# A bidirectional selective scan: one scan instruction for both states of a step, with the seam set up by ScalarE, and GpSimd operands in pairs

## The chip, the cores and the metric

The kernel runs on one core of a Trainium2 chip. A core has five engines with queues of their own: TensorE (PE, matrix products and transposes), VectorE (DVE), ScalarE (ACT), GpSimd (POOL) and SyncE (SP, which here issues DMAs). Each queue is worked off in order; engines wait for each other through semaphores. SBUF is the working memory, 128 partitions wide. PSUM is a smaller one in eight banks of 512 f32 a partition, into which PE writes, and which ACT and DVE read and write too. The metric is the device time of one execution, in microseconds (us).

## The reference, cut to what matters

The input is x of 2 sequences, 2048 tokens, 256 channels, in f32. It passes a layernorm with a modulation, then two Mamba blocks, one forward and one over the reversed sequence, then a mixture of eight experts with a shared one. The change lies in the Mamba blocks alone. Of each, cut:

```
xp, z = split(x @ W_in.T)                    # 512 channels each
xc    = silu(conv(xp) + b_conv)              # 4 taps along the tokens
dt, B, C = split(xc @ W_x.T, [16, 32])       # 16 states: B and C have 16 values a token
dt    = softplus(dt @ W_dt.T + b_dt);  A = -exp(A_log)
step: h = h * exp(dt * A) + (dt * xc) * B    # h: 512 channels x 16 states
      y = sum over the states of h * C
y     = (y + xc * D) * silu(z);  out = y @ W_out.T
```

The recurrence over the tokens is what the kernel's scans compute: for each channel and each state, h[t] = da[t] * h[t-1] + db[t], with da = exp(dt * A) and db = (dt * xc) * B.

## The kernel before, in words

A direction and a sequence are cut in chunks of 512 tokens, which makes 16 chunks (2 directions, 2 sequences, 4 chunks). Channels lie on the partitions in four blocks d of 128; tokens lie along the free axis. The 16 states are taken in eight groups g of two (NG = 2). A *step* is one group of one channel block: two states, 512 tokens each. A chunk has SPC = 32 steps, ordered by pair of blocks p, then g, then block e within the pair; s is the number of a step, over all chunks 0 to 511. Step numbers below are within a chunk.

A step passes these functions:
- `load_b`, `load_c` (SP): rows of B and C of a group, spread over 128 partitions by DMA, once for two steps.
- `inputs` (POOL, L416): db = du * B for both states, 128 x 1024 into a tile of SBUF with ten slots; du is dt * xc (`input_`, L306).
- `decays` (ACT, L435): da = exp(dt * a), one ACTIVATE for each state, 128 x 512 each into a PSUM bank of its own. Even and odd steps have two banks each (`banks`).
- `scans` (DVE, L449): one TENSOR_TENSOR_SCAN for each state, starting from the state `hl` that the chunk before left.
- `weigh_own` (DVE, L455) or `weigh` (POOL, L460): h * C. `on_pool` says which: POOL has the odd blocks but for one group, and steps 4 and 16. For steps on POOL the scan writes h to SBUF; for the others it writes h over the decays in PSUM.
- `carry` (ACT, L470 or L466): the last column of h is copied to hl.
- `sums` (PE, L482): transposes that add up h * C over the states in PSUM; `gate_y` (DVE, L500) multiplies by the gate.

In four *turned* steps of a chunk (6, 7, 18, 19; not in the first chunk) POOL makes no db. PE does it instead, with transposes of scaled du (`scaled`, `operands`, tile op) into the PSUM banks, and the decays go to SBUF.

The order on each engine is written by hand in the loop over s. In one iteration are issued: `load_b`, `weigh(s-2)`, `load_c`, `inputs(s+3)`, `carry(s-1)`, perhaps a softplus, `gate_y(s-5)`, `scans(s)`, `weigh_own(s)`, `decays(s+1)`, `operands(s+1)`, then evacuations of PE's products by ACT (`settle`), `sums(s-4)`, and work for the next chunk that `places` puts at fixed steps (`visit`). Of this, the steps of the prediction touch: the silu of the convolution at step 12 and of the gate at 28 (L242 and L246, each with two table loads on ACT), the product psd at 14 (PE, L253) and its evacuation xd (L258), the four ACTIVATEs ab (L336), the evacuation xT (L209) with the products psx (L219) behind it, and the softplus of the next chunk at steps 20, 22, 24 and 26. A softplus (`softplus_in` on ACT, L292 and L293; `softplus_out` on DVE, L298 to L300) borrows the two PSUM banks of step s+1 before that step's decays are written there.

Of the kernel before, what the change touches and what calls it, by code (L numbers as in the profile page):

```python
# [40 lines left out]
def kernel(  # L41
# [30 lines left out]
    nc.vector.memset(one, 1.0)  # L72

# [4 lines left out]
    def tiled(ap):  # L78

        return ap.rearrange("(j p) c -> p j c", p=P)  # L80

# [16 lines left out]
    with tc.tile_pool(name="mw", bufs=1) as mw, tc.tile_pool(name="mw2", bufs=2) as mw2, \  # L98
# [59 lines left out]
        def on_pool(s):  # L158

            i, _, g, d = steps[s]  # L160
            if i == 0:
                return d % 2 == 1 and g not in (NGR - 4, NGR - 2)
            return s % SPC in (4, 16) or d % 2 == 1 and g != NGR - 2
# [121 lines left out]
        def banks(s, name):  # L285

            return [ps_a.tile([P, TC], F32, tag=f"da{s % 2}_{n}", name=f"{name}_{n}") for n in range(NG)]

        def softplus_in(i, d, s):
            v = ready[i]  # L290
            v["sl"] = banks(s, f"sl{i}_{d}")
            nc.scalar.activation(v["sl"][0], v["e"][:, d, :], AF.Identity, bias=one)  # L292
            nc.scalar.activation(v["sl"][1], v["e"][:, d, :], AF.Ln, bias=one)  # L293

        def softplus_out(i, d):
            v = ready[i]
            (s, ln), e, dt = v["sl"], v["e"][:, d, :], v["dt"][:, d, :]
            nc.vector.scalar_tensor_tensor(e, s, -1.0, e, ALU.add, ALU.subtract)  # L298
            nc.vector.tensor_tensor(ln, ln, e, ALU.subtract)
            nc.vector.scalar_tensor_tensor(dt, dt, 0.0, ln, ALU.max, ALU.add)  # L300
# [111 lines left out]
        def inputs(s):  # L412
            i, _, g, d = steps[s]
            db = m2.tile([P, NG, TC], F32, tag="db", bufs=NDB, name=f"db{s}")
            if not turned_step(s):
                nc.gpsimd.tensor_tensor(db, bc(ready[i]["du"][:, d, :], NG), live["B", s // 2], ALU.mult)  # L416
            live["db", s] = db

        def operands(s):

            if turned_step(s):
                i, _, _, d = steps[s]
                live["op", s] = banks(s, f"op{s}")
                for n, op in enumerate(live["op", s]):
                    for j in range(JC):
                        transpose(op[:, j * P:(j + 1) * P],
                                  ready[i]["ab"][:, n, j, d % 2 * P:(d % 2 + 1) * P], ident)

        def decays(s):
            i, _, g, d = steps[s]  # L430
            w = weights[chunks[i][0]]
            da = [live["db", s][:, n, :] for n in range(NG)] if turned_step(s) else banks(s, f"da{s}")
            for n in range(NG):
                m = g * NG + n
                nc.scalar.activation(da[n], ready[i]["dt"][:, d, :], AF.Exp, scale=w["a"][:, d, m:m + 1])  # L435
            live["da", s] = da

        def scans(s):
            i, _, g, d = steps[s]
            hl, da = state[chunks[i][:2]][0], live.pop(("da", s))  # L440
            x = live.pop(("op", s)) if turned_step(s) else [live["db", s][:, n, :] for n in range(NG)]
            h = x if turned_step(s) else da
            if on_pool(s):
                live["h", s] = m2.tile([P, NG, TC], F32, tag="h", bufs=3, name=f"h{s}")
                h = [live["h", s][:, n, :] for n in range(NG)]
            live["hs", s] = h
            for n in range(NG):
                m = g * NG + n
                nc.vector.tensor_tensor_scan(h[n], da[n], x[n], hl[:, d, m:m + 1], ALU.mult, ALU.add)  # L449

        def weigh_own(s):
            _, _, g, d = steps[s]
            if not on_pool(s):
                for n, h in enumerate(live["hs", s]):
                    nc.vector.tensor_tensor(live["db", s][:, n, :], h, live["C", s // 2][:, n, :], ALU.mult)  # L455

        def weigh(s):
            _, _, g, d = steps[s]
# [3 lines left out]
        def carry(s):  # L462
            i, _, g, d = steps[s]
            hl, hs = state[chunks[i][:2]][0], live.pop(("hs", s))
            if on_pool(s):
                nc.scalar.copy(hl[:, d, g * NG:(g + 1) * NG].unsqueeze(2), live["h", s][:, :, TC - 1:TC])  # L466
            else:
                for n in range(NG):
                    m = g * NG + n
                    nc.scalar.copy(hl[:, d, m:m + 1], hs[n][:, TC - 1:TC])  # L470
# [125 lines left out]
        def load_x(b, q):  # L596
            xt = m2.tile([P, JC, C], F32, tag="db", bufs=NDB, name=f"xt{b}_{q}")
            nc.sync.dma_start(out=xt, in_=tiled(x[b, q * TC:(q + 1) * TC, :]))
            return xt

        def norms(b, q, xt, xn):
# [17 lines left out]
            if xn is None:  # L619
                xn = m2.tile([P, JC, C], F32, tag="db", bufs=NDB, name=f"xo{u}")  # L620
# [20 lines left out]
        front = norms(0, 0, xts[0, 0], xns[0])  # L641
# [39 lines left out]
        def others():  # L681
# [3 lines left out]
            while todo or live:  # L685
                while todo and len(live) < 2:
                    k = todo.pop(0)
                    live.append(norms(*k, xts.pop(k), None))
# [50 lines left out]
        for s in range(3):  # L739
            inputs(s)  # L740
# [28 lines left out]
        for s in range(NST + 4 + SPC):  # L769
# [8 lines left out]
            if s + 3 < NST:  # L778
# [550 lines left out]
```

## Time and profile before

| | us |
|---|---|
| median of 11 runs | 2473.47 (2470.28 to 2479.17) |
| the profiled execution | 2472.45, span 2470.7 |
| first scan starts / last scan ends | 103.3 / 1892.3 |
| a usual chunk, first scan to first scan | 109.2 |
| DVE, POOL, ACT, PE busy in such a chunk | 106.4, 107.3, 85.6, 91.2 |

A group of the profile is a line, an engine, an operation and tiles (out<-in, buffer numbers left out), with the size of one, the count, the busy time in us and the mean duration in ns, then the engine's idle time just before and what ended it. A row of the timeline has start, duration, engine, line, operation and tiles, and in brackets idle time before it and its releaser. The window row has the window, its length, then busy time (and count) of PE, PEld (weight loads), DVE, ACT and POOL, the granted clock of TensorE as a share of full speed, the DMA share and GB/s. Instructions of one engine overlap at their ends, so the sum of durations is above busy time; distances between starts are what an instruction costs in a full queue.

### The profile page before, as it was taken

The page shows a single profiled execution, that of the slowest core. Times are in us where ns is not written, and L with a number is a line of the kernel's source. Part 1 is how long each engine was busy: PE and PEld are TensorE (multiplying, and loading weights), DVE is VectorE, ACT ScalarE, POOL GpSimd, SP SyncE. Part 2 cuts the span into 40 slices and gives each one's busy share as a digit, 9 for nine tenths or more (in the row PEclk, how much of TensorE's full clock was granted, in tenths as well). Part 3 has the DMA queues.
Part 4 walks back from the last instruction along what each step waited for, and adds up shares of the span by engine and source line. Part 5 has one row for each costly group of instructions (what it writes and reads, how often), then busy time and mean ns, then how long its engine had stood idle before and what let it go on. Part 6 is the DMA issues. An engine that isn't in the chain of part 4 may idle for free. (4 is left out here: it accounts for less than half of the span.)

```text
span 2470.7 us, 30346 instructions
## 1 busy us (share of the span) xinstructions
PE 1986.5 (80%) x9512; PEld 1373.3 (56%) x9512; DVE 2031.0 (82%) x2679; ACT 1625.2 (66%) x3377; POOL 1886.0 (76%) x991
## 2 busy tenths in 40 slices
PE   5457879787887879788887978888765487999999
PEld 2134556565555556555555656555555255788885
DVE  5499998999999999999999999999996776322333
ACT  5557787777778787877878777787853235353331
POOL 0367998989999999999999999999996405331304
PEclk9687888898999889899988989899878688999999
DMA  5344448474444454545444544444443501688863
GB/s 165 129 145 146 145 163 252 154 248 166 155 162 164 147 188 165 170 158 167 155 154 163 165 162 152 167 156 148 164 153 99 173 1 63 203 261 239 270 187 102
DMA packets 239974, 403.08 MB, mean 163 GB/s; under 512 B 38818, under 2 KB 171938, under 8 KB 239812
## 3 DMA queue, kind: packets, MB, share of 16 engines
q1 hardware_dynamic: 220724, 370.72, 46.1%
q0 software_dynamic: 6144, 16.79, 2.0%
q10 hardware_dynamic: 12944, 13.64, 1.6%
q8 instruction: 75, 1.23, 0.2%
q14 instruction: 87, 0.71, 0.1%
HBM read 346.54 MB, written 54.53 MB: 162 GB/s over the span
## 5 line engine op out<-in xcount | busy, mean ns | idle before, releaser
L416 POOL TENSOR_TENSOR db<-du,B 128x1024 f32<-128x1024 f32 x452 | 1062.4, 2371 | 13.8 <-DMA B<-bcs 13.8
L460 POOL TENSOR_TENSOR db<-h,C 128x1024 f32<-128x1024 f32 x252 | 597.0, 2370 | 65.8 <-issue 52.6
L435 ACT ACTIVATE da<-dt,w_a 128x512 f32<-128x512 f32 x904 | 594.7, 688 | 76.8 <-DVE dt L300 46.2
L482 PE MATMUL y<-ident,db 128*128 128x128 f32 x4096 | 569.3, 287 | 39.2 <-POOL db L460 36.6
L482 PEld LDWEIGHTS y<-ident,db 128*128 128x128 f32 x4096 | 506.1, 150 | 160.6 <-issue 101.1
L449 DVE TENSOR_TENSOR_SCAN da<-da,hl,db 128x512 f32<-128x512 f32 x460 | 562.8, 1268 | 4.9 <-POOL db L416 3.7
L449 DVE TENSOR_TENSOR_SCAN h<-da,hl,db 128x512 f32<-128x512 f32 x444 | 539.9, 1263 | 15.2 <-ACT da L435 15.2
L455 DVE TENSOR_TENSOR db<-da,C 128x512 f32<-128x512 f32 x460 | 292.1, 676 | 17.7 <-DMA C<-bcs 10.2
L236 PE MATMUL psc<-xp,w_conv 128*128 128x512 f32 x512 | 234.0, 600 | 9.1 <-ACT xp L225 6.4
L219 PE MATMUL psx<-xT,w_in 128*128 128x512 f32 x256 | 156.5, 731 | 103.0 <-ACT hl L470 88.8
L1041 POOL DMA_INDIRECT xs<-xs,slot x64 | 62.4, 975 | 197.2 <-DVE own L1028 95.2
L354 PE MATMUL psz<-w_in,xT 128*128 128x512 f32 x256 | 150.1, 719 | 55.5 <-ACT bT L317 35.7
L1166 POOL DMA_INDIRECT two<-ys,slot x64 | 63.1, 985 | 162.2 <-DVE hs L1068 64.9
L306 POOL TENSOR_TENSOR du<-dt,xc 128x512 f32<-128x512 f32 x64 | 81.7, 1277 | 97.3 <-DVE dt L300 96.7
L236 PEld LDWEIGHTS psc<-xp,w_conv 128*128 128x128 f32 x512 | 93.4, 192 | 106.1 <-issue 95.3
L253 PE MATMUL psd<-xc,w_x 128*48 128x512 f32 x128 | 95.4, 916 | 68.0 <-ACT hl L470 47.5
L219 PEld LDWEIGHTS psx<-xT,w_in 128*128 128x128 f32 x256 | 50.3, 225 | 157.9 <-ACT hl L470 110.8
L382 PE MATMUL pso<-w_out,yg 128*128 128x256 f32 x512 | 118.5, 385 | 22.1 <-ACT e L276 21.9
L1117 DVE COPY gT<-qgT 128x512 f32<-128x512 f32 x46 | 31.8, 692 | 120.5 <-PE qgT L846 120.4
L1062 PE MATMUL pg<-fxT,s 128*128 128x512 f32 x256 | 123.2, 639 | 0.0
L1142 ACT ACTIVATE hT<-qh,bs 128x256 f32<-128x256 f32 x92 | 38.7, 471 | 122.5 <-PE qh L1103 119.7
L382 PEld LDWEIGHTS pso<-w_out,yg 128*128 128x128 f32 x512 | 95.6, 192 | 37.6 <-ACT e L276 25.2
(200 smaller groups left out, 3219.8 us busy)
## 6 DMA issues: line engine op xcount, KB each, us to landing
C<-bcs SPq DMA_DIRECT2D x256, 512.0 KB, 4.4
B<-bcs SPq DMA_DIRECT2D x226, 512.0 KB, 4.3
we<-in_w_dram SPq DMA_DIRECT2D x138, 256.0 KB, 3.7
acc<-acc SPq DMA_DIRECT2D x32, 512.0 KB, 4.9
xs<-ident SPq DMA_DIRECT2D x2, 5888.0 KB, 23.5
xg<-xs SPq DMA_DIRECT2D x46, 256.0 KB, 4.1
ys<-yo ACTq DMA_DIRECT2D x46, 256.0 KB, 3.0
xn<-xn SPq DMA_DIRECT2D x16, 512.0 KB, 5.6
```

What stands on the lines that cost most here:

```text
L219: nc.tensor.matmul(ps, w["in"][:, k, d * P:(d + 1) * P], v["xT"][:, k, :], start=(k == 0), stop=(k == KC - 1))
L236: nc.tensor.matmul(ps, w["conv"][:, d, k, :], v["xp"][:, d, k:k + TC], start=(k == 0), stop=(k == 3))
L253: nc.tensor.matmul(ps[:RK + 2 * NS, :], w["x"][:, d, :], v["xc"][:, d, :], start=(d == 0), stop=(d == ND - 1))
L354: nc.tensor.matmul(ps, v["xT"][:, k, j * P:(j + 1) * P], w["in"][:, k, DI:2 * DI], start=(k == 0), stop=(k == KC - 1))
L382: nc.tensor.matmul(ps[:, n, :], v["yg"][:, d, n * P:(n + 1) * P], wo[:, d, :], start=(d == 0), stop=(d == ND - 1))
L416: nc.gpsimd.tensor_tensor(db, bc(ready[i]["du"][:, d, :], NG), live["B", s // 2], ALU.mult)
L435: nc.scalar.activation(da[n], ready[i]["dt"][:, d, :], AF.Exp, scale=w["a"][:, d, m:m + 1])
L449: nc.vector.tensor_tensor_scan(h[n], da[n], x[n], hl[:, d, m:m + 1], ALU.mult, ALU.add)
L455: nc.vector.tensor_tensor(live["db", s][:, n, :], h, live["C", s // 2][:, n, :], ALU.mult)
L460: nc.gpsimd.tensor_tensor(live["db", s], live.pop(("h", s)), live["C", s // 2], ALU.mult)
L482: nc.tensor.matmul(ys["y"][j // 2][:, j % 2, d % 2 * P:(d % 2 + 1) * P], src[:, j * P:(j + 1) * P], ident, is_transpose=True, start=(first ...
L1062: nc.tensor.matmul(ps, s12[:, n, k, m * P:(m + 1) * P], xTs[b, q][:, k, :], start=(k == 0), stop=(k == KC - 1))
```

## The change

The two PSUM banks of a step become one tile of two states by 512 (`banks`). In steps that are not turned, one scan runs over both states as one row of 1024. So that the second state doesn't go on from the first one's last value, ACT sets up its first token (the seam): it adds da[0] * hl to db[0] there and sets da[0] to zero. For this ACT now reads POOL's db. The second state's decay is issued ahead of the first one's. Weighing on DVE and the carry become one instruction for both states in all steps. POOL makes db of both channel blocks of a pair in one instruction of 128 x 2048, in odd iterations; the ten slots become five of double size, which the layernorm tiles at the start share. The weighing of step 16 goes from POOL to DVE.

```diff
@@ on_pool
-            return s % SPC in (4, 16) or d % 2 == 1 and g != NGR - 2
+            return s % SPC == 4 or d % 2 == 1 and g != NGR - 2
@@ banks
-            return [ps_a.tile([P, TC], F32, tag=f"da{s % 2}_{n}", name=f"{name}_{n}") for n in range(NG)]
+            return ps_a.tile([P, NG, TC], F32, tag=f"da{s % 2}", name=name)
@@ inputs
-            db = m2.tile([P, NG, TC], F32, tag="db", bufs=NDB, name=f"db{s}")
+            i, p, _, d = steps[s]
+            db = m2.tile([P, 2, NG, TC], F32, tag="db", bufs=NDB // 2, name=f"db{s}")
             if not turned_step(s):
-                nc.gpsimd.tensor_tensor(db, bc(ready[i]["du"][:, d, :], NG), live["B", s // 2], ALU.mult)
-            live["db", s] = db
+                nc.gpsimd.tensor_tensor(
+                    db, ready[i]["du"][:, d:d + 2, :].unsqueeze(2).to_broadcast([P, 2, NG, TC]),
+                    live["B", s // 2].unsqueeze(1).to_broadcast([P, 2, NG, TC]), ALU.mult)
+            for e in range(2):
+                live["db", s + e] = db[:, e, :, :]
@@ decays
-            for n in range(NG):
+            da = db if turned_step(s) else banks(s, f"da{s}")
+            for n in reversed(range(NG)):
                 m = g * NG + n
-                nc.scalar.activation(da[n], ready[i]["dt"][:, d, :], AF.Exp, scale=w["a"][:, d, m:m + 1])
+                nc.scalar.activation(da[:, n, :], ready[i]["dt"][:, d, :], AF.Exp,
+                                     scale=w["a"][:, d, m:m + 1])
+            if not turned_step(s):
+                m = g * NG + 1
+                nc.scalar.activation(db[:, 1, 0:1], da[:, 1, 0:1], AF.Identity,
+                                     scale=hl[:, d, m:m + 1], bias=db[:, 1, 0:1])
+                nc.scalar.copy(da[:, 1, 0:1], zero)
@@ scans
-            for n in range(NG):
-                m = g * NG + n
-                nc.vector.tensor_tensor_scan(h[n], da[n], x[n], hl[:, d, m:m + 1], ALU.mult, ALU.add)
+            m = g * NG
+            if turned_step(s):
+                for n in range(NG):
+                    nc.vector.tensor_tensor_scan(h[:, n, :], da[:, n, :], x[:, n, :],
+                                                 hl[:, d, m + n:m + n + 1], ALU.mult, ALU.add)
+            else:
+                h, da, x = (v.rearrange("p n t -> p (n t)") for v in (h, da, x))
+                nc.vector.tensor_tensor_scan(h, da, x, hl[:, d, m:m + 1], ALU.mult, ALU.add)
@@ weigh_own
-                for n, h in enumerate(live["hs", s]):
-                    nc.vector.tensor_tensor(live["db", s][:, n, :], h, live["C", s // 2][:, n, :], ALU.mult)
+                nc.vector.tensor_tensor(live["db", s], live["hs", s], live["C", s // 2], ALU.mult)
@@ carry
-                for n in range(NG):
-                    m = g * NG + n
-                    nc.scalar.copy(hl[:, d, m:m + 1], hs[n][:, TC - 1:TC])
+            nc.scalar.copy(hl[:, d, g * NG:(g + 1) * NG].unsqueeze(2), h[:, :, TC - 1:TC])
@@ the loop
-            if s + 3 < NST:
+            if s % 2 == 1 and s + 3 < NST:
                 inputs(s + 3)
...
```

## The prediction

> **What bounds the kernel now.** I read the page first, for the share of each engine and the 40 slices.
>
> ```profile
> PE 1986.5 (80%) x9512; PEld 1373.3 (56%) x9512; DVE 2031.0 (82%) x2679; ACT 1625.2 (66%) x3377; POOL 1886.0 (76%) x991
> ...
> DVE  5499998999999999999999999999996776322333
> ACT  5557787777778787877878777787853235353331
> POOL 0367998989999999999999999999996405331304
> ```
>
> The scan stage is slices 2 to 31 (scans run from 103 to 1892 us). Both DVE and POOL are full there, so the page can't say which sets the pace. One chunk can: its first scan starts at 1029.74 us and the next chunk's at 1138.93, and most chunks take 109.2 us. Busy time by engine in that window:
>
> ```profile
> 1029.74:1138.93 109.19, 91.15 (x462) 60.55 (x461) 106.36 (x115) 85.61 (x179) 107.28 (x49) 0.91 0.49 165
> ```
>
> DVE (third sum, 106.36) idles 2.8 us, POOL (fifth) 1.9, ACT (fourth) 23.6. The waits of this window give DVE's idle time: 1.28 us at one scan on a decay (ACT), 0.8 and 0.2 at the scans fed by transposes, 0.27 in a softplus, the rest in gaps of 0.03. POOL waits 1.1 and 0.8 us for a DVE scan. So DVE sets the pace, with POOL and ACT arriving just in time. The groups give the prices:
>
> ```profile
> L416 POOL TENSOR_TENSOR db<-du,B 128x1024 f32<-128x1024 f32 x396 | 930.5, 2370 | 11.9 <-DMA B<-bcs 11.9
> L435 ACT ACTIVATE da<-dt,w_a 128x512 f32<-128x512 f32 x792 | 521.3, 688 | 68.2 <-DVE dt L300 41.7 <-DVE e L298 26.1
> L449 DVE TENSOR_TENSOR_SCAN h<-da,hl,db 128x512 f32<-128x512 f32 x398 | 483.7, 1263 | 13.4 <-ACT da L435 13.4
> L455 DVE TENSOR_TENSOR db<-da,C 128x512 f32<-128x512 f32 x396 | 251.4, 675 | 10.2 <-DMA C<-bcs 10.2
> L470 ACT COPY hl<-da 128x1 f32<-128x1 f32 x398 | 53.0, 158 | 53.8 <-DVE db L455 51.2
> ```
>
> Durations overlap by some 0.08 us in a row, so I use distances of starts: two scans 2.35, two weighings (L455) 1.18. Since DVE hardly ever waits for a decay, what matters is how late a decay could come. The timelines of ACT and DVE show three places with almost no room. First, steps 10 to 17, which hold the silu and its two table loads:
>
> ```profile
> 1063.84 1.31 ACT L435 ACTIVATE da<-dt,w_a 128x512 f32<-128x512 f32 x2
> ...
> 1067.93 1.28 ACT L242 ACT_TABLE_LOAD   x1
> ...
> 1072.65 1.30 ACT L435 ACTIVATE da<-dt,w_a 128x512 f32<-128x512 f32 x2
> ...
> 1081.97 0.58 ACT L258 COPY xd<-psd 48x512 f32<-48x512 f32 x1 [3.23 <-PE psd L253]
> ...
> 1082.55 1.30 ACT L435 ACTIVATE da<-dt,w_a 128x512 f32<-128x512 f32 x2
> ```
>
> DVE in the same stretch, weighing 10 and scan 17:
>
> ```profile
> 1062.48 1.26 DVE L455 TENSOR_TENSOR db<-da,C 128x512 f32<-128x512 f32 x2
> ...
> 1083.34 2.46 DVE L449 TENSOR_TENSOR_SCAN h<-da,hl,db 128x512 f32<-128x512 f32 x2 [1.28 <-ACT da L435]
> ```
>
> Second, the softplus hand-overs (four a chunk), where the next step's decays reuse the softplus banks:
>
> ```profile
> 1096.90 0.69 DVE L300 SCALAR_TENSOR_TENSOR dt<-dt,sl 128x512 f32<-128x512 f32 x1
> ...
> 1097.50 1.28 DVE L455 TENSOR_TENSOR db<-da,C 128x512 f32<-128x512 f32 x2
> 1097.62 0.69 ACT L435 ACTIVATE da<-dt,w_a 128x512 f32<-128x512 f32 x1 [0.77 <-DVE dt L300]
> ...
> 1098.70 1.27 DVE L449 TENSOR_TENSOR_SCAN h<-da,hl,db 128x512 f32<-128x512 f32 x1
> ```
>
> Third, the silu of the gate in steps 28 to 30:
>
> ```profile
> 1126.05 0.19 ACT L466 COPY hl<-h 128x2 f32<-128x2 f32 x1 [0.49 <-DVE h L449]
> ...
> 1132.17 1.30 ACT L435 ACTIVATE da<-dt,w_a 128x512 f32<-128x512 f32 x2
> ```
>
> **The change, part by part.** The sum is made against the profiled execution, 2472.45 us (span 2470.7), 1.0 below the median of the runs.
>
> *One scan of 1024 for two of 512* (28 of 32 steps; turned steps keep two). Scans of 8, 128 and 512 elements take 0.174, 0.424 and 1.263 us: 2.08 ns an element between the first two, 2.19 between the last two. So 1024 take 2.33 to 2.38 us, a distance of 2.25 to 2.30, and a step saves 0.05 to 0.11. I take 0.06, from the nearer sizes. *One weighing for two:* a TENSOR_TENSOR of 1024 takes 1.22 us (L1176), distance 1.14: saves 0.04.
> *Weighing of step 16 from POOL to DVE:* DVE +1.14, POOL -2.32 a chunk. It falls before scan 17, which waits 1.28 us for ACT today, so its cover is that wait.
> *POOL in pairs:* 512 elements take 1.28 us, 1024 2.37, so 2048 about 4.56, distance 4.50 for 4.64. With step 16 POOL falls from 107.3 to about 103 us a chunk. That is worth nothing while ACT makes DVE wait. A pair's slot comes free with PE's sums of its second step, which at step 20 stand behind the psd product (1075.49 to 1081.94); POOL may wait there, with the room it has gained.
> *Carries:* one copy of two columns where own steps had two copies; ACT saves some 0.06.
> *The seam:* an ACTIVATE with pointers for scale and bias and a copy, both one column, behind the two decays of a step. No row shows this ACTIVATE. The copy of one column (L470) is followed after 0.06 and takes 0.16. Two pointers cost 0.18 of both: L209 with two is followed after 0.66, L374, a plain copy of the same size, after 0.48. So I take 0.24 for the ACTIVATE and 0.06 for the copy. The lower end is the copy's own 0.06 for both; the upper end is no overlap at all, 0.34 and 0.16. ACT's busy time has room for 28 of these; its delay has not.
>
> The scan now needs both decays and the seam, where the first half needed one decay. From the first decay's start that was 0.69 and 0.10 of hand-over (1082.55 to 1083.34). Now it is 0.62 + 0.61 + 0.24 + 0.16 + 0.10 = 1.73, 0.94 later. In a plain step there is room: decays start 0.1 after a weighing ends, DVE then has a 2.29 us scan. In the three places there is none:
>
> Steps 10 to 17: from the end of weighing 10 (1063.74) to scan 17 (1083.34) 19.60 us pass, on ACT and PE alone: decays, silu, decays, four ab, the psd product, xd, decays. On this path lie three seams (0.90), two saved copies (-0.12) and the later scan (0.94): +1.72. DVE itself needs 19.60 - 1.28 - 6 x 0.06 - 3 x 0.04 + 1.14 = 18.98, so weighing 16 is free, but nothing is gained.
> Softplus: scan 21 starts 1.11 us after L300 ends (1097.59). Both decays now wait for L300, since the second state's goes first: 0.03 + 1.73 = 1.76. +0.65 four times, +2.60. Queued behind the decays on ACT are the evacuations of PE's banks and the next carry, all with room.
> Steps 28 to 30: one seam and one copy less (+0.24) put decays 30 at 1132.41, scan 30 at 1134.14 where it starts at 1133.02 now: +1.12.
> Step 6: its scan waits 0.80 us for transposes at the end of an unbroken PE stretch that begins with psx behind the evacuation xT (ACT, step 30). That moves by only 0.24 + two seams = 0.84, so -0.30 against +1.12; what DVE gains from step 31 to 5 goes into this wait.
> Left as gains: scans 8 to 10 and 20 to 27, 11 x 0.06, four weighings x 0.04, the 0.2 at scan 18: -1.02.
> A chunk: 1.72 + 2.60 + 1.12 - 0.30 - 1.02 = +4.12. The cheap seam with 0.11 a scan gives +1.8 (1.00 + 1.88 + 0.82 - 0.30 - 1.57); the dear one with 0.05 a scan +6.2 (2.5 + 3.3 + 1.6 - 0.3 - 0.9).
>
> Chunks 1 to 14 count as 13, as 2 and 3 (114.6 and 112.9 us, DMA waits of C and B) cover part: +53.6. The first chunk has six softplus hand-overs, +3.9; its first pair of operands is 2.2 us later, under a wait of 7.5 us before the first weighing (113.29). The last chunk has neither silu nor softplus: -1.2. What follows at 1892 us is untouched. Sum +56: 2472.45 + 56 = 2528.8, as a median 2529.
>
> The pages, which the sum doesn't use: the Trainium skill, "ScalarE: Activation LUTs", section "What ACT_TABLE_LOAD costs", speaks against the change: an ACTIVATE costs 186 ns plus 0.833 per element, each pointer operand 93 more, and neighbours overlap by 93, so one column is nearly all fixed cost. By it (my estimate) the pair occupies 0.37 us and a chunk loses 4.8. "VectorE: DVE Perf Modes", section on the TRN2 errata, speaks for it: each instruction pays about 150 cycles once, so a merged scan would save 0.156 and not the 0.06 of the rows, 1.1 us more a chunk, as long as ACT is on time.
>
> **The rivals.**
> *ACT stays in time, and the change is faster.* If the scan can start as early as DVE is free, a chunk gains 28 x 0.06 for scans and, with weighing 16 in the 1.28 us that stood idle, 1.28 - 1.14 + 16 x 0.04: -2.5, with 0.11 a scan -3.9; over 14 chunks 2438 to 2418. For it: ACT has 23.6 us idle a chunk. It decides at the softplus hand-over: decays and seam would have to end within 1.05 us of L300, and two decays alone take 1.3. Chance 0.09.
> *POOL's pair is dear.* The seam makes ACT wait for POOL's product, and behind it on ACT stand PE's evacuations, the carry and the next decays. From weighing 3 to pair 16 POOL runs six weighings and five pairs, 36.4 us, for the 38.0 that DVE takes from the end of scan 3 (1041.62) to scan 16 (1079.63) now. From about 4.7 us a pair it makes ACT wait; at 5.1 the five give +2 more a chunk, 2557. Against it: broadcast and plain operands cost the same today (L416 and L460, 2.37). Chance 0.08.
> *No difference:* the seam at the lower end, and DVE waits half hidden: less than +10, 2473 to 2483. Chance 0.05.
>
> **How the numbers follow.** The likeliest case, ACT late at three places, has 0.78, its own range 2497 (1.8 a chunk) to 2558 (6.2). Range: 2488 to 2556, cutting the thin upper end and most of the last rival. 0.2% (5 us) is about what can be told from no change. Slower: 0.78 + 0.08 + 0.03; same 0.02; faster 0.1.
>
> **What would show it.** Scans of 1024 near 2.35 us long; waits of some 0.65 us on ACT before scans 21, 23, 25 and 27, and of 1 us or more at 14, 17 and 30; POOL waiting more for DVE; a chunk of about 113 us. Wrong if those scans start without a wait, if pairs exceed 4.7 us, or if the seam's ACTIVATE is followed within 0.1 us.

## The result, and the profile after

The kernel after takes 2654.71 us (median of 8 runs, 2652.61 to 2656.70) against 2473.89 for the kernel before (31 runs): a ratio of 1.0731, 95% interval 1.0721 to 1.0740. It is slower, as forecast, but by 181 us where the forecast had 56, and 2654.71 lies far above the range of 2488 to 2556.

From the page of the kernel after, the shares of the engines and the 40 slices of the span (2654.4 us):

```profile
PE 2041.8 (77%) x9512; PEld 1410.1 (53%) x9512; DVE 2029.5 (76%) x1983; ACT 1878.7 (71%) x4021; POOL 1820.6 (69%) x750
...
DVE  5488888888888888898888888898989577422333
ACT  5667888888888888888888888888886243454331
POOL 0367888788888878888988888888889411430404
```

DVE has as much to do as before (2029.5 us against 2031.0), but most of its slices have fallen from 9 to 8, and POOL's too: both now wait. ACT has gained 253.5 us of work and shows an even row of 8. The same is seen in one chunk, here the tenth (number 9, counted from 0), from its first scan to the next chunk's:

```profile
1246.99:1368.00 121.01, 95.61 (x462) 63.40 (x461) 106.42 (x71) 101.14 (x220) 103.02 (x33) 0.85 0.43 144
```

The third sum, DVE's, is the 106.4 us of before; the chunk is 121.0 long instead of 109.2. ACT (fourth) has 101.1 instead of 85.6, POOL (fifth) 103.0 instead of 107.3. TensorE's granted clock in the window is 0.85 instead of 0.91, but the products psd, which lie on the path of steps 10 to 17, take 0.88 us each in the mean of the scan stage, against 0.93 before, so the loss on that path isn't theirs. What DVE waited for in that window says who holds it up (us in total, times, longest):

```profile
DVE da L468 <- ACT da L450: 5.5, 5, 2.1
DVE h L468 <- ACT da L450: 4.4, 5, 0.9
DVE op L464 <- PE op L177: 1.5, 1, 1.5
DVE e L303 <- ACT sl L298: 1.3, 1, 1.3
```

Ten scans wait for L450, the copy that ends the seam. In this chunk the scans of steps 21, 23, 25 and 27 wait 0.93 to 0.95 us each, those of 14 and 30 about 2.1. The groups of the scan stage, by shape, give the new prices:

```profile
L422 POOL TENSOR_TENSOR db<-du,B 128x2048 f32<-128x2048 f32 x194 | 880.0, 4539 | 14.1 <-DMA B<-bcs 14.1
...
L468 DVE TENSOR_TENSOR_SCAN da<-da,hl,db 128x1024 f32<-128x1024 f32 x208 | 489.2, 2352 | 89.1 <-ACT da L450 79.6 <-ACT hl L481 2.1 <-POOL db L422 1.0
...
L472 DVE TENSOR_TENSOR db<-da,C 128x1024 f32<-128x1024 f32 x208 | 254.3, 1223 | 12.9 <-DMA C<-bcs 3.9
L448 ACT ACTIVATE db<-da,db,hl 128x1 f32<-128x1 f32 x385 | 135.3, 351 | 25.1 <-ACT da L444 1.1 <-POOL db L422 0.9
```

The pair of POOL takes 4.54 us (worked: 4.56), the scan 2.35 (2.33 to 2.38), the weighing 1.22: all as priced, and so is the copy with 0.16 (rows below). The seam's ACTIVATE takes 0.35, and how it stands in the queue is the point on which the sum failed. A softplus hand-over in the timeline of ACT (x2 is two instructions in one row, from the first one's start to the second one's end):

```profile
1319.48 1.42 ACT L444 ACTIVATE da<-dt,w_a 128x512 f32<-128x512 f32 x2 [2.73 <-DVE dt L305]
1320.93 0.35 ACT L448 ACTIVATE db<-da,db,hl 128x1 f32<-128x1 f32 x1
1321.32 0.16 ACT L450 COPY da<-zero 128x1 f32<-128x1 f32 x1
1321.41 0.15 ACT L481 COPY hl<-da 128x2 f32<-128x2 f32 x1
1321.60 1.42 ACT L444 ACTIVATE da<-dt,w_a 128x512 f32<-128x512 f32 x2
```

and of DVE:

```profile
1318.76 0.69 DVE L305 SCALAR_TENSOR_TENSOR dt<-dt,sl 128x512 f32<-128x512 f32 x1
1319.36 1.22 DVE L472 TENSOR_TENSOR db<-da,C 128x1024 f32<-128x1024 f32 x1
1321.51 2.35 DVE L468 TENSOR_TENSOR_SCAN h<-da,hl,db 128x1024 f32<-128x1024 f32 x1 [0.93 <-ACT da L450]
```

The two decays together take 1.42 us, where they took 1.30 before: the second starts 0.72 after the first instead of 0.62. The ACTIVATE of the seam starts 0.03 *after* they end, and the copy 0.04 after the ACTIVATE's end: nothing up to the copy overlaps any more. From the first decay's start to the scan 2.03 us pass (1.42 + 0.03 + 0.35 + 0.04 + 0.16 + 0.03); the sum had 1.73. And from the start of this step's decays to the next step's, ACT needs 2.12 us with the carry.

Where the 183.6 us between the two profiled spans lie: the first scan starts 4.9 us later (108.2 against 103.3), the first chunk is 9.4 longer, chunks 1 to 14 together 163.6 (11.7 each), the last chunk 2.2 up to the start of its last scan, and what follows from there 3.5.

### The profile page after: what moved, and what is told of

The parts are those of the page before. It is cut to its first block, busy times and chain, and to the rows that moved or that the text cites. A ratio compares the mean times of both kernels' runs of the same rounds, so it can differ in the third digit from the quotient of the medians.

```text
span 2654.4 us, 29632 instructions
## 1 busy us (share of the span) xinstructions
PE 2041.8 (77%) x9512; PEld 1410.1 (53%) x9512; DVE 2029.5 (76%) x1983; ACT 1878.7 (71%) x4021; POOL 1820.6 (69%) x750
## 3 DMA queue, kind: packets, MB, share of 16 engines
q8 instruction: 75, 1.23, 0.2%
## 5 line engine op out<-in xcount | busy, mean ns | idle before, releaser
L422 POOL TENSOR_TENSOR db<-du,B 128x2048 f32<-128x2048 f32 x226 | 1025.9, 4543 | 15.6 <-DMA B<-bcs 15.5
L476 POOL TENSOR_TENSOR db<-h,C 128x1024 f32<-128x1024 f32 x237 | 560.2, 2366 | 307.2 <-issue 245.7
L444 ACT ACTIVATE da<-dt,w_a 128x512 f32<-128x512 f32 x904 | 626.3, 693 | 110.9 <-DVE dt L305 87.6
L468 DVE TENSOR_TENSOR_SCAN da<-da,hl,db 128x1024 f32<-128x1024 f32 x245 | 576.2, 2352 | 105.9 <-ACT da L450 94.8
L493 PE MATMUL y<-ident,db 128*128 128x128 f32 x4096 | 591.1, 295 | 35.7 <-POOL db L476 30.3
L493 PEld LDWEIGHTS y<-ident,db 128*128 128x128 f32 x4096 | 526.7, 154 | 158.3 <-issue 108.9
L468 DVE TENSOR_TENSOR_SCAN h<-da,hl,db 128x1024 f32<-128x1024 f32 x207 | 483.7, 2342 | 63.9 <-ACT da L450 63.9
L472 DVE TENSOR_TENSOR db<-da,C 128x1024 f32<-128x1024 f32 x245 | 299.6, 1223 | 19.2 <-DMA C<-bcs 8.3
L448 ACT ACTIVATE db<-da,db,hl 128x1 f32<-128x1 f32 x452 | 158.8, 351 | 36.5 <-POOL db L422 8.3
L359 PEld LDWEIGHTS psz<-w_in,xT 128*128 128x128 f32 x256 | 56.1, 242 | 151.9 <-DVE acc L390 56.9
```

Of the source, the lines that this page charges most:

```text
L359: nc.tensor.matmul(ps, v["xT"][:, k, j * P:(j + 1) * P], w["in"][:, k, DI:2 * DI], start=(k == 0), stop=(k == KC - 1))
L422: nc.gpsimd.tensor_tensor(db, ready[i]["du"][:, d:d + 2, :].unsqueeze(2).to_broadcast([P, 2, NG, TC]), live["B", s // 2].unsqueeze(1).to_b ...
L444: nc.scalar.activation(da[:, n, :], ready[i]["dt"][:, d, :], AF.Exp, scale=w["a"][:, d, m:m + 1])
L448: nc.scalar.activation(db[:, 1, 0:1], da[:, 1, 0:1], AF.Identity, scale=hl[:, d, m:m + 1], bias=db[:, 1, 0:1])
L468: nc.vector.tensor_tensor_scan(h, da, x, hl[:, d, m:m + 1], ALU.mult, ALU.add)
L472: nc.vector.tensor_tensor(live["db", s], live["hs", s], live["C", s // 2], ALU.mult)
```

## The experiments

Times of each run stand beside runs of the kernel before on the same chip. Chunk means are over chunks 7 to 14 (counted from 0) of the profiled run, first scan to first scan; before has 109.2, after 120.9.

| kernel | ratio [95%] | median, before beside it | chunk | first chunk |
|---|---|---|---|---|
| before | 1 | 2473.47 | 109.2 | 155.4 |
| after | 1.0731 [1.0721, 1.0740] | 2654.71, 2473.89 | 120.9 | 164.8 |
| no_seam | 1.0232 [1.0215, 1.0249] | 2530.82, 2474.17 | 112.5 | 156.6 |
| one_tile | 1.0361 [1.0344, 1.0378] | 2563.66, 2474.17 | 114.3 | 163.2 |
| one_decay | 1.0037 [1.0023, 1.0051] | 2482.66, 2474.17 | 109.1 | 153.0 |
| pairs_16 | 1.0049 [1.0032, 1.0066] | 2486.78, 2474.17 | 109.2 | 157.4 |
| seam_aside | 1.0396 [1.0370, 1.0423] | 2613.14, 2514.86 | 115.7 | 158.9 |
| zero_only | 1.0327 [1.0302, 1.0352] | 2595.13, 2514.86 | 114.1 | 159.6 |
| swap_22 | 0.9950 [0.9932, 0.9968] | 2502.46, 2514.86 | 107.7 | 155.6 |
| swap_26 | 0.9969 [0.9956, 0.9982] | 2505.75, 2514.86 | 108.0 | 155.4 |
| one_decay_seam | 1.0431 [1.0415, 1.0447] | 2581.08, 2475.35 | 115.7 | 160.2 |
| pool_undone | 1.0732 [1.0715, 1.0748] | 2655.65, 2475.35 | 121.2 | 168.3 |
| pairs_22_26 | 0.9969 [0.9958, 0.9980] | 2467.47, 2475.35 | 108.2 | 155.0 |

The four runs from seam_aside to swap_26 shared a chip on which the kernel before itself took 2514.86 us. No trace of the kernel before was kept there; in the traces of the four, 621 to 626 us pass from the start of the last scan to the end, where the trace of before has 581, which is about the difference. For these four, the ratios and the chunks are compared, not the medians.

Two theories stood against each other. The first: ACT's instructions of a step wait for each other, because they now share one tile of PSUM, and this makes the chain to the scan longer than worked out. The second: the two instructions of the seam cost what they cost by taking ACT's time. Beside these stood the other parts of the change, the merged scan and POOL's pairs.

### Without the seam

The seam's ACTIVATE and copy are left out, so that the second state goes on from the first one's last value.

```diff
-            if not turned_step(s):
-                m = g * NG + 1
-                nc.scalar.activation(db[:, 1, 0:1], da[:, 1, 0:1], AF.Identity,
-                                     scale=hl[:, d, m:m + 1], bias=db[:, 1, 0:1])
-                nc.scalar.copy(da[:, 1, 0:1], zero)
```

> The changed kernel without the seam: the two ACT instructions of one column are left out, so the second state of a step starts from the first one's end instead of its own. A usual chunk took 109.2 us before and 120.9 after. Theory 1 (waits inside one tile): as the two states of a step now share one PSUM tile, each instruction on it waits for the end of the one before even on its own engine; the second decay starts 0.72 us after the first instead of 0.62, and the weighing 0.09 after the end of its scan. These waits stay without the seam; the chunk stays above 115 us, the kernel above 2560. Theory 2 (the seam itself): its 0.35 and 0.16 us, with the waits of 0.03 to 0.09 around them, make up most of the 11.7 us a chunk; without it a chunk takes about 112 us, the kernel 2500 to 2525.

A chunk takes 112.5 us and the run 1.0232 of before. Of the 11.7 us a chunk that the change costs, 8.4 go with the seam and 3.3 stay. The first theory in its plain form, that the shared tile does most of it by itself, falls; the second had 112 us a chunk, but 2500 to 2525 in all, and 2531 is above it. So the seam does most, and not all. What stays need not be the shared tile alone: here too one scan waits for both decays, and this run doesn't separate the two.

### The kernel before, with its two banks made one tile

```diff
-            return [ps_a.tile([P, TC], F32, tag=f"da{s % 2}_{n}", name=f"{name}_{n}") for n in range(NG)]
+            v = ps_a.tile([P, NG, TC], F32, tag=f"da{s % 2}", name=name)
+            return [v[:, n, :] for n in range(NG)]
```

> The kernel before, with one edit: the two PSUM banks of a step become one tile. Scans, weighings, carries, POOL and the computation are as before. Theory 1 (waits inside one tile) expects the second scan, the weighings and the second decay each to wait some 0.1 us for their own engine: 32 x 0.12 and 16 x 0.12 us on DVE, and some 0.4 us at each of the four softplus hand-overs, 6 to 9 us a chunk, 2560 to 2610 in all. Theory 2 (the seam itself) expects at most 1 us a chunk, 2473 to 2490.

This one declaration costs 3.6% [3.4, 3.8], 5.1 us a chunk, with every instruction of the kernel before kept; 2564 us lies at the lower edge of what the first theory expected (2560), and 5.1 us a chunk is less than its 6 to 9. A step of ACT in the timeline of this kernel:

```profile
1127.24 1.42 ACT L436 ACTIVATE da<-dt,w_a 128x512 f32<-128x512 f32 x2
```

and the scans and weighings of a step on DVE:

```profile
1125.71 2.62 DVE L450 TENSOR_TENSOR_SCAN da<-da,hl,db 128x512 f32<-128x512 f32 x2 [0.19 <-ACT da L436]
1128.36 1.29 DVE L456 TENSOR_TENSOR db<-da,C 128x512 f32<-128x512 f32 x2
```

The pair of decays takes the same 1.42 us as in the kernel after. On DVE the two scans take 2.62 (2.60 in the median) where a pair that writes to PSUM took 2.44 before, and the weighings start 0.03 after them. So two instructions of one engine that write the halves of one PSUM tile run one after the other here, although the halves lie in two banks. Scans that only read the halves and write h to SBUF take 2.45 a pair in both kernels. Nor is it so in SBUF: in the turned steps the decays go to two halves of one tile in SBUF, and there the second starts 0.62 after the first, as in the kernel before.

The instructions' semaphores in the trace say where the order comes from. In one_tile all 452 second decays into PSUM wait for a semaphore that ACT itself raises, and each time it was last raised some 0.02 us before they start. Of the 452 in the kernel before, 258 name that semaphore, but it was last raised 0.51 us or more before the start, so it held up none of them. Of the 60 into SBUF none names it, in either kernel. So the lost overlap is a wait that stands in the program once the two buffers are one tile; whether the chip would need it isn't shown.

The change pays this price on ACT; on DVE it merges the two instructions that would pay it.

### One decay for both states

The two decays become one ACTIVATE of 1024, with no seam. The second state's own rate and its own start are left out.

```diff
-            for n in reversed(range(NG)):
...
+                nc.scalar.activation(da, bc(ready[i]["dt"][:, d, :], NG), AF.Exp, scale=w["a"][:, d, m:m + 1])
```

> The changed kernel without the seam, and with one ACTIVATE of 1024 elements for both decays of a step (the second state's own rate and its own start are left out). A row of 1024 on ACT takes 1.06 us, so decays come earlier than the two of 1.25 before, and what is left is DVE's own time. If the merged scan and weighing save DVE time, as the prediction had it (0.06 and 0.04 us each), and weighing 16 hides, the chunk falls to 106 to 108 us, 2430 to 2460. If the weighing's wait for its scan takes the saving back (scan to weighing 2.45 us in the trace after, weighing 1.14: 3.59 for 3.53 before), it stays at 108 to 110.5, 2460 to 2495.

The chunk is 109.1 us, that of the kernel before, as the second of the two expectations had it. Everything else of the change is in this kernel, the merged scan, the merged weighing, the single carry, POOL's pairs and step 16 on DVE, and it neither gains nor loses a chunk's worth. DVE's timeline says why the merging gains nothing:

```profile
1130.74 2.35 DVE L466 TENSOR_TENSOR_SCAN h<-da,hl,db 128x1024 f32<-128x1024 f32 x1
1133.01 2.33 DVE L466 TENSOR_TENSOR_SCAN da<-da,hl,db 128x1024 f32<-128x1024 f32 x1
1135.43 1.23 DVE L470 TENSOR_TENSOR db<-da,C 128x1024 f32<-128x1024 f32 x1
1136.57 2.35 DVE L466 TENSOR_TENSOR_SCAN da<-da,hl,db 128x1024 f32<-128x1024 f32 x1
```

A scan behind which an independent scan stands is followed after 2.27 us, 0.08 less than the 2.35 of two half scans, more than the 0.06 forecast. But a scan followed by its own weighing costs 2.42: the weighing reads what the scan has just written and waits for its end, where before the first half's weighing stood behind the second half's scan and started early. Scan and weighing together take 2.42 + 1.14 = 3.56, a step of before 3.53.

### POOL's part alone

The kernel before, with POOL's pairs and with weighing 16 on DVE.

```diff
-            return s % SPC in (4, 16) or d % 2 == 1 and g != NGR - 2
+            return s % SPC in (4,) or d % 2 == 1 and g != NGR - 2
...
+            db = m2.tile([P, 2, NG, TC], F32, tag="db", bufs=NDB // 2, name=f"db{s}")
...
-            if s + 3 < NST:
+            if s % 2 == 1 and s + 3 < NST:
                 inputs(s + 3)
```

> The kernel before with only the POOL part of the change: operands of both channel blocks in one instruction, and the weighing of step 16 on DVE. Theory 1 and 2 both have POOL off the path: 2466 to 2478, weighing 16 under the wait before scan 17. The rival that pairs land too late, or that weighing 16 costs DVE its 1.18 us a chunk: 2490 to 2510.

The chunk stays at 109.2: pairs and weighing 16 are free in it, and bring nothing. The median lies between the two expectations (up to 2478, from 2490). The medians differ by 12.6 us, the profiled spans by 16.9, and these lie elsewhere: the first scan starts 3.8 later, the first chunk is 2.0 longer, chunks 1 to 5, some of which wait for DMAs, 7.1 together, the last chunk 1.2, the part behind it 2.4.

### The seam's two instructions, on a tile that nobody waits for

```diff
...
-                nc.scalar.activation(db[:, 1, 0:1], da[:, 1, 0:1], AF.Identity,
-                                     scale=hl[:, d, m:m + 1], bias=db[:, 1, 0:1])
-                nc.scalar.copy(da[:, 1, 0:1], zero)
+                nc.scalar.activation(scratch[:, s % 4, 0:1], eps, AF.Identity, scale=one, bias=eps)
+                nc.scalar.copy(scratch[:, s % 4, 1:2], zero)
```

The seam itself is left out by this, and ACT's work is kept.

> The changed kernel, with the two one-column ACT instructions of each step turned to a scratch tile of their own: the same ACT work, but neither waits for the decays or POOL, and no scan waits for them (the second state starts from the first one's end). A usual chunk takes 120.9 us with the seam and 112.6 without. Theory 1 (the seam's cost is the chain of waits: 0.03 to 0.09 + 0.35 + 0.03 + 0.16 between a decay's end and its scan): without waits the two cost ACT about 0.3 us a step, off most scans' path, a chunk 113 to 115, 2535 to 2565. Theory 2 (ACT's own time for two more instructions, wherever they point): 118 to 121, 2610 to 2655.

A chunk of 115.7 and a ratio of 1.0396: between the two, by the chunk 0.7 us above what the first theory expected and 2.3 below the second's. Against no_seam, ACT's time for two more instructions costs 3.2 us a chunk; against after, their place in the chain, with the waits that it brings, costs 5.2. ACT's timeline of this kernel also tells how the seam runs when it waits for nothing:

```profile
1201.70 1.42 ACT L445 ACTIVATE da<-dt,w_a 128x512 f32<-128x512 f32 x2
1203.06 0.37 ACT L449 ACTIVATE scratch<-eps,one 128x1 f32<-128x1 f32 x1
1203.34 0.17 ACT L450 COPY scratch<-zero 128x1 f32<-128x1 f32 x1
1203.42 1.56 ACT L342 ACTIVATE ab<-psu,bT 128x256 f32<-128x256 f32 x4
```

It starts 0.06 before the decays end, the ACTIVATE is followed after 0.28 and the copy after 0.08. The forecast had 0.24 and 0.06. So the prices of the rows were right for instructions that don't depend on each other, and the seam's do.

### The copy alone

The seam's ACTIVATE is left out, the copy of zero kept, so that the second state starts from db alone.

```diff
-                nc.scalar.activation(db[:, 1, 0:1], da[:, 1, 0:1], AF.Identity,
-                                     scale=hl[:, d, m:m + 1], bias=db[:, 1, 0:1])
                 nc.scalar.copy(da[:, 1, 0:1], zero)
```

> The changed kernel without the seam's ACTIVATE; the copy that zeroes the second state's first decay stays (the state carried from the chunk before is left out for the second state). The copy adds 0.03 of wait and 0.16 to the way from the second decay to the scan, of 0.57 to 0.63 for the whole seam. Theory 1 (cost follows the length of the chain): a third of the 8.3 us, a chunk of 115 to 115.8, 2562 to 2580. Theory 2 (cost by instruction, or a fixed price of an instruction that waits on its own engine): a half, 116.5 to 117.5, 2585 to 2605.

A chunk of 114.1, below both expectations (115 and more): 1.6 us a chunk over no_seam for the copy, and so 6.8 for the ACTIVATE.

### One decay, with the seam

One ACTIVATE of 1024 for both decays as in one_decay, and the seam behind it. The second state's own rate is left out. By the durations of the runs above this makes the chain about as long as the forecast's 1.73 us.

> The changed kernel with one ACTIVATE of 1024 elements for both decays (the second state's own rate is left out) and with the seam. From the start of the decay to the scan ACT then needs 1.06 + 0.03 + 0.35 + 0.03 + 0.16 + 0.10 = 1.73 us, which is the length that the prediction worked with, where the changed kernel itself shows 2.0 to 2.1; ACT's time of a step is 1.65 for the prediction's 1.55 and 1.95. Theory 1 (the prediction's places and rule were right, the length of the chain was wrong): the chunk comes near the predicted +4.1, 112.5 to 114.5 us for 120.9, the kernel 1.030 to 1.045 of before. Theory 2 (the sum over places was wrong too, lateness costs more than the waits at the ends of chains): still above 116, 1.055 or more.

In the timeline of ACT:

```profile
1282.44 1.12 ACT L448 ACTIVATE da<-dt,w_a 128x1024 f32<-128x1024 f32 x1 [1.70 <-DVE dt L305]
1283.59 0.35 ACT L451 ACTIVATE db<-da,db,hl 128x1 f32<-128x1 f32 x1
1283.97 0.16 ACT L453 COPY da<-zero 128x1 f32<-128x1 f32 x1
```

and the scan that it releases, on DVE:

```profile
1284.17 2.35 DVE L471 TENSOR_TENSOR_SCAN h<-da,hl,db 128x1024 f32<-128x1024 f32 x1 [0.63 <-ACT da L453]
```

From the decay's start to the scan 1.73 us pass (1.12 + 0.03 + 0.35 + 0.03 + 0.16 + 0.04), and the wait at the hand-over is 0.63, where the forecast had 0.65. So this kernel shows what the forecast's argument gives when its chain is granted: 6.5 us a chunk, not 4.1. Its chunk of 115.7 lies between the two expectations, its ratio within the first. The last 5.2 up to after come with a chain that is 0.30 us longer, 1.42 for two decays instead of 1.12 for one. These also take 0.30 us more of ACT's time in each step, and this run doesn't tell the two apart; seam_aside showed that ACT's time alone has a price too.

### The change with POOL's part undone

Ten slots of one step, `inputs` once a step, weighing 16 on POOL, and the rest of the change kept.

```diff
-            return s % SPC == 4 or d % 2 == 1 and g != NGR - 2
+            return s % SPC in (4, 16) or d % 2 == 1 and g != NGR - 2
...
-            if s % 2 == 1 and s + 3 < NST:
+            if s + 3 < NST:
                 inputs(s + 3)
```

> The changed kernel with POOL's part undone: operands step by step, and the weighing of step 16 on POOL again. If POOL's part costs nothing in a chunk because DVE waits for ACT there anyway (the prediction's view, and pairs_16's 109.2), a chunk stays at 120 to 121 us and the kernel within 0.8% of the changed one's 1.073, a little better from the start (pairs_16 lost 12 us, at the start and in the first chunks): 1.066 to 1.073. If pairs that land late feed ACT's lateness, 1.05 or less.

The same time as after, at the upper edge of what was expected by its ratio, and with 121.2 us a chunk (120 to 121 expected). The first scan comes at 104.9 instead of 108.2, but the first chunk is 3.5 us longer. With pairs_16 this settles POOL's part: in a usual chunk it is off the path in both kernels.

### The weighings of steps 16 and 22 (or 26) exchanged between DVE and POOL

The kernel before, with the weighing of step 16 on DVE, as in the change, and that of step 22 (or 26) on POOL in return, so that neither engine has more to do.

```diff
-            return s % SPC in (4, 16) or d % 2 == 1 and g != NGR - 2
+            return s % SPC in (4, 22) or d % 2 == 1 and g != NGR - 2
```

> The kernel before with one edit: the weighing of step 16 goes from POOL to DVE and that of step 22 from DVE to POOL. From the runs so far: a weighing at step 16 fills the 1.28 us that DVE waits there for ACT (pairs_16: chunk unchanged at 109.2), and at step 22, a softplus step, POOL catches up with DVE. If that holds, a chunk takes 108.0 and the kernel 2454 to 2462. If POOL, at 107.2 us of 109.2, becomes the bound, or scan 23 then waits for its decays: 2472 to 2480.

> As swap_22, with step 26 instead of 22: later in the chunk, where POOL has caught up further but little time is left until weighings 27 and the next chunk. Expected 2454 to 2462 by the same account; 2472 or more if POOL's lag then carries into the next chunk.

Step 22 moved gives 0.9950 [0.9932, 0.9968], the lowest ratio of all kernels here, though its interval overlaps those of the next two, and at the edge of what was expected; step 26 moved gives 0.9969 [0.9956, 0.9982], a smaller gain than expected. The window of a chunk of swap_22:

```profile
1136.96:1244.17 107.21, 88.19 (x459) 59.41 (x458) 106.16 (x115) 85.54 (x179) 107.14 (x49) 0.93 0.48 163
```

This chunk is as long as POOL is busy (107.14), and DVE (106.16) has 1 us left; over chunks 7 to 14 the means are 107.7, 106.9 and 106.2. This uses the one idle place on DVE that the change had found, the wait before scan 17, without the seam: that wait is gone in all but the first of these chunks. From scan 22 to scan 23 pass 4.77 us where it was 5.97, since its own weighing no longer stands between the softplus and the next scan.

### Pairs, and two weighings given to POOL

The kernel before with POOL's pairs from the second chunk on, weighing 16 on DVE, and those of 22 and 26 on POOL.

```diff
+            return s % SPC in (4, 22, 26) or d % 2 == 1 and g != NGR - 2
...
+            if i == 0:
+                for e in range(2):
+                    nc.gpsimd.tensor_tensor(db[:, e, :, :], bc(ready[i]["du"][:, d + e, :], NG),
+                                            live["B", s // 2], ALU.mult)
+            elif not turned_step(s):
```

> The kernel before, with operands in pairs from the second chunk on, and the weighings of step 16 moved to DVE and of 22 and 26 to POOL. swap_22 took 107.7 us a chunk for 109.2, with DVE busy 105.2 and POOL 107.2. Pairs save POOL 2 us, weighing 26 costs it 2.3 and saves DVE 1.2. If POOL bounds, 107.5 a chunk, a ratio of 0.99 to 0.995, no better than swap_22; if DVE does, 106.5 and 0.985 to 0.99. If the pairs cost at the start even so, as in pairs_16: above 0.995.

0.9969 [0.9958, 0.9980], 108.2 us a chunk: better than before, no better than swap_22 with its smaller edit, and a smaller gain than both expectations for a chunk without a price at the start (107.5 and 106.5). The time that pairs save on POOL went into a second weighing, and POOL is again the engine with the least room, 0.8 us idle a chunk where DVE has 3.0.

## Why the prediction was right, and where it failed

The differences to before by stretches of a chunk, from scan start to scan start (us, means over chunks 7 to 13), beside what the forecast's terms say for the same stretch; its gains are put where it had them:

| scans | forecast | one_decay | no_seam | one_decay_seam | after |
|---|---|---|---|---|---|
| 30 to 6 | -0.30 | -0.24 | +0.40 | +0.50 | +1.32 |
| 6 to 8 (turned) | 0 | +0.30 | +0.23 | +0.30 | +0.42 |
| 8 to 10 | -0.18 | -0.13 | -0.13 | -0.14 | +0.09 |
| 10 to 17 | +1.72 | -0.14 | +0.81 | +1.55 | +3.08 |
| 17 to 20 | -0.20 | +0.31 | -0.02 | -0.12 | -0.19 |
| 20 to 28 (softplus) | +1.96 | -0.39 | +1.17 | +3.00 | +4.79 |
| 28 to 30 | +1.12 | +0.19 | +0.78 | +1.40 | +2.17 |
| chunk | +4.12 | -0.11 | +3.24 | +6.50 | +11.67 |

- **What bounds before and where there is no room: right.** The three places named, steps 10 to 17, the softplus and steps 28 to 30, carry 10.0 of the 11.7 us.
- **The chain from the first decay to the scan, 0.62 + 0.61 + 0.24 + 0.16 + 0.10 = 1.73: this step failed.** It measured 2.03 and, in steps of even number, 2.15. The failed terms are the decays (1.45 from the first one's start to the seam's, instead of 1.23) and the ACTIVATE (0.39 to the copy's start instead of 0.24); the hand-over to DVE was dearer on paper, 0.10 for 0.03, and the copy right. On ACT the same terms make a step longer by some 0.4 us. Distances of instructions that don't depend on each other were used for instructions that do. The upper end, "no overlap at all, 0.34 and 0.16", named this very case for the seam, and its 0.34 was measured as 0.35; I took the nearer rows and not the end that the dependence between the instructions would have pointed to. The loss of overlap between the two decays was in neither end, so that the own range's 6.2 a chunk was too low. One_decay_seam shows the price: with the chain at 1.73 the stretch 10 to 17 comes out at +1.55 (forecast 1.72) and the hand-over wait at 0.63 (0.65). The step from there to after, longer chain and longer ACT time together, is 5.2 of the 7.6 us a chunk that were missed.
- **"ACT's busy time has room for 28 of these; its delay has not": half right.** seam_aside shows that two instructions with no delay to the scan cost 3.2 us a chunk as well. ACT's idle time lies ahead of the hand-overs (2.73 us in the row shown), where it waits for DVE, and not behind them, where decays, seam and carry of two steps follow each other without a gap.
- **The gains of 1.02: not there.** The merged scan saves 0.08 where an independent scan follows, and loses it where its own weighing follows; one_decay, with all the rest of the change, ends at -0.11 a chunk. The weighing of 16 is free, as forecast, and gains nothing.
- **Step 6, -0.30: wrong in sign.** Its wait for transposes grew from 0.8 to 1.5 us in the chunk shown (1.7 in the mean), and the stretch 30 to 6 lost 1.32. Of this, 0.43 is the joined tile. PE's transposes and DVE's scan, before and after:

```profile
1047.62 1.04 PE L172 MATMUL op<-ident,ab 128*128 128x128 f32 x8
1048.32 1.29 DVE L449 TENSOR_TENSOR_SCAN op<-db,hl,op 128x512 f32<-128x512 f32 x1 [0.80 <-issue]
...
1265.01 1.04 PE L177 MATMUL op<-ident,ab 128*128 128x128 f32 x8
1266.14 2.61 DVE L464 TENSOR_TENSOR_SCAN op<-db,hl,op 128x512 f32<-128x512 f32 x2 [1.50 <-PE op L177]
```

  Before, the first scan starts 0.70 us after the first transpose, with its own four done; after, 1.13, behind all eight, as in one_tile. The transposes themselves end 0.88 later in the mean, which is the rest. The products psx ahead of them wait for ACT (99.5 us in the scan stage against 81.7 before); that this is ACT's lateness alone isn't shown.
- **A wait not foreseen:** the softplus of step 22 (L303) waits 1.26 us for its ACTIVATE L298, whose place on ACT is behind the seams of the steps ahead; it was 0.27 before and is 0.61 in no_seam. It is part of the 4.79 of the stretch 20 to 28.
- **The first pair of operands "under a wait of 7.5 us": wrong, and small.** The first scan came 4.9 us later in after and 3.8 in pairs_16. In the pool_undone kernel it came 1.6 later, and the first chunk took the difference back.
- **What would show it.** The scans are 2.35 us long. The waits before scans 21, 23, 25 and 27 are 0.93 and not 0.65, those before 14 and 30 over 1 us as said; before 17 there is none or up to 0.7, as the loss came at 14 already. POOL idles 18 us in the chunk shown instead of 1.9, which its waits don't put down to DVE, and the chunk is 121 us long and not 113. The seam's ACTIVATE is not followed early, so the sign that would have made the forecast too high did not show.
- **The rivals.** ACT in time falls by the waits. POOL's pairs are dear falls by 4.54 us a pair, by pairs_16 and by pool_undone. No difference falls by the result.

The rule set against the rows: the Trainium skill, "ScalarE: Activation LUTs", section "What ACT_TABLE_LOAD costs", gives 186 ns, 0.833 an element and 93 for each pointer operand, and has neighbours overlap by 93 ns; worked out from this, an estimate, the seam's ACTIVATE takes 0.373 us. The trace has 0.351 for it and, where it depends on the decay, no overlap; independent, in seam_aside, it is followed 0.28 after its start, which is the page's 0.373 - 0.093. The page was the better price, and it too had the overlap that a dependence takes away. "VectorE: DVE Perf Modes", section on the TRN2 errata, has some 150 cycles once an instruction; the estimate from it, 0.156 us saved by a merged scan, is not reached: 0.08 was measured, in the favourable order alone.

What stays open: whether the chip itself needs the waits between instructions of one engine at one PSUM tile. Taking the waits away inside the tile wasn't tried, nor were decays in SBUF for all steps, where the turned steps show no such wait. Nor was it separated how much of the 5.2 us is the scan's later start and how much ACT's lost time, or why the seam's ACTIVATE starts 0.09 us behind the decays in steps of even number and 0.03 in the others.

## What to carry to other kernels

Price a chain of short instructions that wait for each other by their full durations plus the gaps that the trace shows, here 0.03 to 0.1 us, and not by distances between independent neighbours; here this took the chain from 1.73 to 2.03 us, and 0.3 us in 28 steps, on the path and in ACT's time, cost 5.2 us a chunk. Joining two buffers into one tile so that one instruction can span them also joined their waits here: one_tile paid 3.6% for the declaration before any instruction had changed. When an engine's idle time lies in a few long stretches, added instructions are paid in the full stretches: ACT idled 23.6 of 109.2 us, and two instructions a step that no scan waits for still cost 3.2 us a chunk. The cheap edit was to move work into the idle place itself, as swap_22 did.

## What was not expected of the hardware

- Two ACTIVATEs of 128x512 into the halves of one PSUM tile of two banks start 0.72 us apart, into two tiles or into halves of an SBUF tile 0.62. A pair of scans that write such halves takes 2.60 us instead of 2.44. The Trainium skill, "PSUM — Partial Sum Buffer", section "PSUM bank collisions raise a hardware error", asks for guards between two different engines at one bank; these waits join one engine's instructions at two banks, which that rule doesn't ask for, and the trace has them as semaphore waits of the program.
- A weighing that reads the scan just ahead of it starts 0.03 to 0.09 us after its end, and an independent scan 0.08 before: the order of two instructions on DVE is worth 0.1 us or more.
- One ACTIVATE of 1024 takes 1.12 us, two of 512 in separate tiles 1.30, two in one tile 1.42: fewer, longer instructions were the gain on ACT, where both states could share one pointer.
